# Moving three weight loads and the exponentials within the opening convolution of a residual-block kernel

## The chip, the cores and the metric

The kernel runs on one core of a Trainium2 chip. The metric is the device time of one execution in microseconds (us). The figure for a version is the median of its runs.

## What is computed

The input x has 32 batches of 64 rows of 1024 float32 values. Four layers are added to it, one after the other. `id0` to `id3` are integers, one per batch.

```python
# 0: a long convolution along the 1024 values, one filter K[h] per row h, cut at a length per batch
P = dtA[:, :, None] * arange(1024)               # 64 rows x 64 complex states x 1024 positions
K = 2 * einsum('hn,hnl->hl', Ct, exp(P)).real    # the 64 filters
x = x + mask(id0) * (causal_conv(x, K) + x * D[:, None])
# 1 and 2: a 1024x1024 matrix per batch, chosen among 16
x = x + einsum('bsi,boi->bso', x, w1[id1])
x = x + einsum('bij,bkj->bik', x, w2[id2])
# 3: a gated feed-forward layer (1024 -> 2752 -> 1024) with low-rank additions chosen per batch
x = x + down(silu(gate(x)) * up(x))
```

## The kernel before

**Stages.** The rows of x are cut into 4 chunks of 8 batches (512 tokens). The kernel first does the whole of layer 0 for all batches (`convolution`, L1128 to L1445); the part of it that belongs to the first chunk is added to x in SBUF, the rest is written to DRAM (`cd`). Then layers 1 and 2 follow for the first chunk (`adapter`, L297): each of its 16 pairs of layer and batch needs 8 weight tiles of 128x1024 float32 (0.52 MB each), 128 in all. Then come the feed-forward layer of chunk 0, and the other chunks.

**The filters.** They are made on the chip in nine groups of 4, 4, 8, 8, ... rows (`GROUPS`). Position is split as 32 a + b, and a filter is a small matmul of one factor for `a` with another for `b`. For a group g, `kernels(g)` (L1311) does this:

- GpSimd multiplies out the exponents (`rho`) and the angles (`r`) (`powers`, L1224).
- ScalarE (ACT) takes the exponential of rho (`sizes`, L1241).
- VectorE (DVE) brings the angles into the sine's range (`reduced`, L1172).
- ACT takes the cosine as an Abs and a Sin (`cosine`, L1181), and two more sines (L1324, L1326). Exponential and sine need different function tables, and a table load stands between them.
- DVE multiplies sizes, sines and factors together: `et` and `gt`; the last product is L1336.
- TensorE (PE) makes the filters from them (`pk`, L1341 and L1350), ACT copies these out (`ks`, L1359), and ACT's DMA queue stores them to DRAM (`kp`, L1361).

Two groups are made ahead. The third is started in the middle of the first four rows, and so on: while `convolve` works on a group, the second group after it is made (`more`, L1437). The tile scheduler lays the instructions of all engines out from its own estimate of times, and a `tc.issue_after(i)` puts what stands within it behind instruction i. `behind(done, g)` (L1237) does so for the g-th instruction of a list, or does nothing where g is out of range. In the version before, the exponentials of groups 2 and 3 stand behind the store of group 1 (L1244); those of later groups have no such rule.

**The convolution.** `convolve` (L1367) takes four rows at a time, "a four" (16 fours; the four at row 44 is `ha = 44`). The queue of SyncE (SP) issues its DMAs in order:

- `uf`: the inputs of the four (0.52 MB, two buffers), L1371.
- `hk`: the filters of the first two rows as Toeplitz tiles, read from `kp` with overlapping rows (1.05 MB, three buffers), L1380.
- then weights of the adapter stage by `fetch`, L1389.
- `hk` of the other two rows (the second half-four), and again weights.

PE multiplies each half-four in 16 matmuls of two passes (`pc`, L1396, 32 records in the profile); in the middle of some fours the small `pk` matmuls of a later group come between (`between()`, L1392). DVE masks the result into `tmp` (L1403), GpSimd adds the first chunk's part to x (L1411) and writes the rest to `cd` (L1414, L1415).

**Weights ahead.** `first_weights` (L178) lists 36 of the adapter stage's 128 weight tiles that have a buffer before that stage begins: 9 of the rotating pool, 20 in their own places, 7 in places that become free when the last filters are made. Each `next` on it issues one. Eight go out with the first four (`FIRST_LOADS`, L1373), one with every later four, and a second one with each of the last five (`MORE_LOADS = 5`). The remaining 8 follow behind the last four.

Of the kernel before, what the change touches and what calls it, by code (L numbers as in the profile page):

```python
# [11 lines left out]
AF = mybir.ActivationFunctionType  # L12
# [8 lines left out]
B, H, L = 32, 64, 1024  # L21
# [14 lines left out]
LEFT_AT = 11  # L36
LATE = 7
FIRST_LOADS = 8
MORE_LOADS = 5
ROTATING = 9  # L40
HA = 4
SEG = 2
# [1085 lines left out]
def convolution(tc, cst, consts, xt, xf, ssm, lens, x0, cd, ps_tile, fetch, places):  # L1128
# [10 lines left out]
    nc = tc.nc  # L1139
    with ExitStack() as ctx:  # L1140
# [27 lines left out]
        def tt(o, a, b, op):  # L1168
            nc.vector.tensor_tensor(o, a, b, op)
            return o  # L1170

        def reduced(theta, k):  # L1172

            nc.vector.tensor_scalar(k, theta, 1.0 / TWO_PI, MAGIC, ALU.mult, ALU.add)
            nc.vector.tensor_scalar(k, k, MAGIC, None, ALU.subtract)
            for part in (C1, C2, C3):
                nc.vector.scalar_tensor_tensor(theta, k, -part, theta, ALU.mult, ALU.add)  # L1177
            nc.vector.tensor_scalar(theta, theta, PI_IN, -PI_IN, ALU.min, ALU.max)
            return theta

        def cosine(o, r, k):  # L1181

            nc.scalar.activation(k, r, AF.Abs)
            nc.scalar.activation(o, k, AF.Sin, scale=-1.0, bias=col(CO_HALF))
# [27 lines left out]
        def big(g, tag, pool, pairs):  # L1212

            n = GROUPS[g]
            t = pool.tile([P, (1 + pairs) * HG * LQ], F32, tag=f"b{tag}", name=f"b{tag}{g}")
            if pairs:
                return t[:, : 2 * n * LQ].rearrange("p (i h l) -> p i h l", i=2, h=n)
            return t[:, : n * LQ].rearrange("p (h l) -> p h l", h=n)

        def over_l(g, ap):  # L1220
            h0, n = sum(GROUPS[:g]), GROUPS[g]
            return ap[:, h0 : h0 + n].unsqueeze(2).to_broadcast([P, n, LQ])

        def powers(g, v, pool, tag):  # L1224

            o = big(g, tag, pool, True)
            for i in range(2):
                at_ = cst[:, CO_LVAL + i * LQ : CO_LVAL + (i + 1) * LQ]
                at_ = at_.unsqueeze(1).to_broadcast([P, GROUPS[g], LQ])
                with behind(raised, len(raised) - 1 if g > 1 else -1):  # L1230
                    last = nc.gpsimd.tensor_tensor(o[:, i], over_l(g, v), at_, ALU.mult)
            raised.append(last.ins)
            return o

        sized, made, raised, stored = [], [], [], []

        def behind(done, g):  # L1237

            return tc.issue_after(done[g]) if 0 <= g < len(done) else ExitStack()

        def sizes(g):  # L1241
            rho = powers(g, x, s2, "rho")

            with behind(stored, 1 if g in (2, 3) else -1):  # L1244
                done = nc.scalar.activation(rho, rho, AF.Exp)
            sized.append(done.ins)
            return rho
# [5 lines left out]
        nc.vector.scalar_tensor_tensor(x, ea, -1.0, dt, ALU.mult, ALU.mult)  # L1253
        tt(y, aim, dt, ALU.mult)
        rhos = {g: sizes(g) for g in range(2)}

        t, em, ep = small(), small(), small()
# [29 lines left out]
        re, im = slice(0, NS), slice(NS, P)  # L1287
# [23 lines left out]
        def kernels(g):  # L1311

            h0, n = sum(GROUPS[:g]), GROUPS[g]
            rho = rhos.pop(g) if g in rhos else sizes(g)
            r = powers(g, y, s2, "r")
            k, co = big(g, "k", s1, True), big(g, "co", s1, True)

            with tc.issue_after(made[0]) if g == 1 else ExitStack():
                reduced(r, k)
            si = big(g, "si", s1, False)  # L1320

            with behind(stored, g - 1 if g < 3 else -1):
                cosine(co, r, k)
                nc.scalar.activation(si, r[:, 0], AF.Sin)  # L1324

                nc.scalar.activation(co[im, 1], r[im, 1], AF.Sin)  # L1326
            gt, et = big(g, "gt", s2, False), big(g, "et", s2, False)
            if g == 1:
                done = nc.gpsimd.tensor_tensor(et, co[:, 1], rho[:, 1], ALU.mult)
                raised.append(done.ins)  # L1330
            else:
                tt(et, co[:, 1], rho[:, 1], ALU.mult)
            tt(co[:, 0], co[:, 0], over_l(g, fc), ALU.mult)
            tt(si, si, over_l(g, fs), ALU.mult)
            tt(si, si, co[:, 0], ALU.add)
            done = nc.vector.tensor_tensor(gt, si, rho[:, 0], ALU.mult)  # L1336
            made.append(done.ins)

            ps = ps_tile(f"pk{g}")[:LQ, : n * LQ].rearrange("a (h b) -> a h b", b=LQ)
            for i in range(n):  # L1340
                nc.tensor.matmul(  # L1341
                    ps[:, i],
                    gt[:, i, :],
                    et[:, i, :],
                    start=(i == 0),
                    stop=False,
                    skip_group_check=True,
                )

            nc.tensor.matmul(  # L1350
                ps[:, :, 0],
                cst[:, CO_SEL : CO_SEL + LQ],
                dskip[:, h0 : h0 + n],
                start=False,
                stop=True,
                skip_group_check=True,
            )
            ks = s2.tile([LQ, HG, LQ], F32, tag="ks", name=f"ks{g}")
            nc.scalar.copy(ks[:, :n], ps)  # L1359
            kp = kps[h0 : h0 + n]  # L1360
            done = nc.scalar.dma_start(  # L1361
                kp[:, P:].rearrange("h (a b) -> a h b", b=LQ), ks[:, :n]
            )
            stored.append(done.ins)
            return kp

        def convolve(kp, row, ha, between):  # L1367


            uf = s3.tile([P, HA, KT, B], F32, tag="uf", name=f"uf{ha}", bufs=2)  # L1370
            nc.sync.dma_start(uf, xf[:, ha : ha + HA])  # L1371
            if ha == 0:
                fetch(FIRST_LOADS)  # L1373
            tmp = g0_2.tile([P, HA, KT * B], F32, tag="tmp", name=f"tmp{ha}")
            for i in range(0, HA, 2):
                hk = s3.tile([P, 2, L], F32, tag="hk", name=f"hk{ha + i}")

                for j in range(0, 2, 1 if ha == 0 else 2):
                    n = 1 if ha == 0 else 2
                    nc.sync.dma_start(  # L1380
                        hk[:, j : j + n],
                        bass.AP(
                            tensor=kps.tensor,
                            offset=kp[row + i + j : row + i + j + 1, 1:2].offset,
                            ap=[[1, P], [KROW, n], [1, L]],
                        ),
                    )

                if ha and (i == 0 or ha >= H - HA * MORE_LOADS):  # L1389
                    fetch(1)  # L1390
                if i:
                    between()  # L1392
                ps = ps_tile(f"pc{ha + i}").rearrange("p (i t) -> p i t", i=2)
                for j in range(2):
                    for d in range(KT):
                        nc.tensor.matmul(  # L1396
                            ps[:, j, d * B :],
                            hk[:, j, d * P : (d + 1) * P],
                            uf[:, i + j, : KT - d, :].rearrange("p k b -> p (k b)"),
                            start=(d == 0),  # L1400
                            stop=(d == KT - 1),
                        )
                tt(  # L1403
                    tmp[:, i : i + 2, :],
                    ps,
                    maskf.unsqueeze(1).to_broadcast([P, 2, KT * B]),
                    ALU.mult,
                )
            xv = x0.rearrange("p k (b h) -> p k b h", h=H)[:, :, :, ha : ha + HA]
            tv = tmp.rearrange("p i (k b) -> p k b i", b=B)[:, :, :BC, :]  # L1410
            nc.gpsimd.tensor_tensor(xv, xv, tv, ALU.add)  # L1411
            co = g0.tile([P, NCK - 1, HA * KT, BC], F32, tag="co", name=f"co{ha}")
            tv = tmp.rearrange("p i (k c b) -> p c (i k) b", k=KT, b=BC)[:, 1:]
            nc.gpsimd.tensor_copy(co, tv)  # L1414
            nc.gpsimd.dma_start(  # L1415
                cd.rearrange("c p g e -> p c g e")[:, :, ha // HA],
                co.rearrange("p c i b -> p c (i b)"),
            )


        ready = [kernels(0), kernels(1)]

        lnf = g0.tile([P, B], F32, tag="lnf", name="lnf")
# [187 lines left out]
```

## Time and profile before

| | |
|---|---|
| median of 3 runs | 2308.88 us (2307.97 to 2309.78) |
| profiled execution, and its span | 2305.76 us, 2304.1 us |
| PE busy | 2244.8 us, 97% of the span |
| DVE, ACT, POOL (GpSimd) busy | 1322.2, 379.5, 272.3 us |
| moved by DMA | 684.96 MB, mean 297 GB/s |
| first and last matmul of the convolution (L1396) | 29.2 and 189.2 us |
| PE in L1396 | 151.2 us, 1024 records, mean 309 ns of one |
| landing of an hk (34 DMAs) | 5.5 / 8.8 / 10.4 us, min / median / max |
| chain that ended last | PE 80%, DMA 11%, DVE 4%, issue 3% |

The page cuts the span into 40 equal slices of 57.6 us; a digit is the busy share of an engine in tenths, and the line of GB/s is what DMA moved. A timeline has one instruction or a run of like ones to a line: its start, its time, the engine, the line of the code, what it writes from what, how many; in brackets is how long the engine stood idle before it, and what ended that. A table of stretches has, for each stretch, its length, then the busy us and number of instructions of PE, PEld (weight loads of PE), DVE, ACT and POOL, and then the granted clock of PE, the share of DMA and its GB/s. `SPq` and `ACTq` are the DMA queues of SP and ACT.

### The profile page before, as it was taken

Reading aid. Unit: us, or ns where it says so; the run is one execution under the profiler, and the core shown is the slowest. Engines: PE = TensorE matmul, PEld = TensorE weight load, DVE = VectorE, ACT = ScalarE, POOL = GpSimd, SP = SyncE. Lnnn points to the kernel's source line nnn. Section 1 sums busy time; section 2 is a strip of 40 time slices with the busy share of each in tenths; the row PEclk is TensorE's granted clock in tenths of the full one; section 3 lists DMA queues with packets and bytes.
Section 4 is the critical chain, followed back from the end, with each engine's and each line's share of the span. In section 5 each row is a group of like instructions: output and inputs, shape, how many; then the busy total and the mean of one; then the engine's idle time right before and its main releaser. Section 6 shows DMA issues by size and latency. Waiting matters only on the chain.

```text
span 2304.1 us, 53703 instructions
## 1 busy us (share of the span) xinstructions
PE 2244.8 (97%) x21690; PEld 1863.6 (81%) x21690; DVE 1322.2 (57%) x2791; ACT 379.5 (16%) x822; POOL 272.3 (12%) x388
## 2 busy tenths in 40 slices
PE   4999989999999999999999999999999999999999
PEld 4996557787677789688779889688779889799998
DVE  7511138577447776546535676546535676477585
ACT  4300001011001112122102212122002212121220
POOL 4423004112001221000000011000000011100000
PEclk9999999999999999999999999999999999999999
DMA  8999998889988947889998957889998947285582
GB/s 295 373 389 397 407 387 291 315 303 359 362 322 310 350 161 272 298 290 362 359 348 292 361 154 282 297 298 357 359 330 300 361 148 278 90 292 203 195 278 68
DMA packets 201802, 684.96 MB, mean 297 GB/s; under 512 B 26178, under 2 KB 28482, under 8 KB 201042
## 3 DMA queue, kind: packets, MB, share of 16 engines
q1 hardware_dynamic: 169714, 590.77, 69.9%
q0 software_dynamic: 25184, 82.37, 9.6%
q10 hardware_dynamic: 6656, 8.39, 1.0%
q8 instruction: 171, 2.80, 0.5%
q14 instruction: 77, 0.63, 0.1%
HBM read 614.02 MB, written 67.40 MB: 296 GB/s over the span
## 4 chain that ended last, share of the span: by engine, by line
PE 80%; DMA 11%; DVE 4%; issue 3%; POOL 1%; ACT 0%; SPq 0%; POOLq 0%; ACTq 0%; DVEq 0%
PE pq L662 29%; PE po L1061 23%; PE pa L304 12%; DMA wa<-in_w 7%; PE pf L571 6%; PE pc L1396 5%; PE pr L795 3%; PE pe L454 2%; DMA sums<-kept 1%; DMA wa<-sums 1%; DMA hk<-kp 1%; PE pl_d L425 1%; DVE br L1177 0%; DMA wr<-in_wr 0%; DMA wf<-in_wg 0%
## 5 line engine op out<-in xcount | busy, mean ns | idle before, releaser
L304 PE MATMUL pa<-wa,x 128*32 128x256 f32 x7760 | 447.8, 380 | 18.2 <-DMA wa<-in_w 16.0
L662 PE MATMUL pq<-xd,wa 128*128 128x128 f32 x3360 | 415.6, 275 | 0.4
L304 PEld LDWEIGHTS pa<-wa,x 128*32 128x32 f32 x7760 | 241.6, 110 | 208.1 <-DMA wa<-in_w 48.2
L662 PEld LDWEIGHTS pq<-xd,wa 128*128 128x128 f32 x3360 | 394.9, 192 | 1.1 <-DMA wa<-sums 1.1
L662 PE MATMUL pq<-xd,wb 128*128 128x128 f32 x2520 | 324.1, 276 | 0.1
L662 PEld LDWEIGHTS pq<-xd,wb 128*128 128x128 f32 x2520 | 300.7, 192 | 4.0 <-DMA wb<-parts 0.3
L314 DVE STREAM_TRANSPOSE y<-pa 128x512 f32<-128x512 f32 x64 | 45.9, 716 | 284.0 <-PE pa L304 275.2
L1061 PE MATMUL po<-act,wd 128*128 128x256 f32 x640 | 168.6, 386 | 0.0
L1061 PE MATMUL po<-actd,s 128*128 128x256 f32 x640 | 164.4, 379 | 0.0
L1061 PE MATMUL po<-actd,wd 128*128 128x256 f32 x640 | 164.3, 379 | 0.0
L353 POOL DMA_INDIRECT bgu<-in_bgu,rows x44 | 52.5, 1193 | 915.1 <-PE pe L454 823.6
L1396 PE MATMUL pc<-uf,hk 128*128 128x256 f32 (+7 forms) x1024 | 151.2, 309 | 8.2 <-DMA hk<-kp 7.0
L1396 PEld LDWEIGHTS pc<-uf,hk 128*128 128x128 f32 x1024 | 146.4, 192 | 12.5 <-DMA hk<-kp 5.0
L571 PE MATMUL pf<-xd,wf 128*128 128x256 f32 x640 | 150.6, 381 | 0.0
L1061 PEld LDWEIGHTS po<-act,wd 128*128 128x128 f32 x640 | 117.8, 190 | 29.9 <-issue 14.6
L480 DVE TENSOR_TENSOR s<-wd 128x256 f32<-128x256 f32 x80 | 33.8, 423 | 182.8 <-PE po L1061 182.6
L1061 PEld LDWEIGHTS po<-actd,s 128*128 128x128 f32 x640 | 121.5, 190 | 16.7 <-DVE s L481 0.3
L1061 PEld LDWEIGHTS po<-actd,wd 128*128 128x128 f32 x640 | 121.6, 190 | 16.5
L571 PEld LDWEIGHTS pf<-xd,wf 128*128 128x128 f32 x640 | 120.8, 190 | 17.2
L1093 ACT COPY uo<-po 128x256 f32<-128x256 f32 x48 | 17.9, 372 | 623.7 <-PE po L1061 621.6
L571 PE MATMUL pf<-xd,s 128*128 128x256 f32 x480 | 114.4, 381 | 2.9 <-DVE act L605 1.6
L571 PEld LDWEIGHTS pf<-xd,s 128*128 128x128 f32 x480 | 90.3, 190 | 18.4 <-DVE act L605 3.6
(235 smaller groups left out, 2567.4 us busy)
## 6 DMA issues: line engine op xcount, KB each, us to landing
wa<-in_w SPq DMA_DIRECT2D x485, 512.0 KB, 7.2
wa<-sums SPq DMA_DIRECT2D x210, 512.0 KB, 5.8
wb<-parts SPq DMA_DIRECT2D x120, 384.0 KB, 5.4
wd<-in_wd SPq DMA_DIRECT2D x80, 512.0 KB, 7.0
wb<-in_wq SPq DMA_DIRECT2D x90, 384.0 KB, 6.2
hk<-kp SPq DMA_DIRECT2D x30, 1024.0 KB, 8.9
sums<-kept POOLq DMA_DIRECT2D x30, 1024.0 KB, 7.3
wf<-in_wg SPq DMA_DIRECT2D x20, 512.0 KB, 6.6
```

The source lines that it names most:

```text
L304: nc.tensor.matmul(acc[i * S : (i + 1) * S, s * 256 : (s + 1) * 256], xs[c][:, kt, lo + s * S : lo + (s + 1) * S], wt[:, i * 256 : (i + 1) ...
L314: nc.vector.transpose(y, acc)
L353: nc.gpsimd.indirect_dma_start(out=t, out_offset=None, in_=table, in_offset=bass.IndirectOffsetOnAxis(ap=at_, axis=0),)
L425: nc.tensor.matmul(ps[pair(j)], at[:, i, pair(j)], x_i[:, 2 * H * j : 2 * H * (j + 1)], start=(i == 0), stop=(i == n - 1),)
L454: nc.tensor.matmul(ps[:, at_ * 2 * H : (at_ + 1) * 2 * H], bt[pair(j), g], tms[table][pair(j)], start=(g == 0), stop=True, skip_group_chec ...
L480: nc.vector.tensor_add(s1, a21, a22)
L571: nc.tensor.matmul(ps, ws[j][:, kt, :], xb[j][:, kt, :], start=start and kt == 0, stop=kt == KH - 1, skip_group_check=True,)
L662: nc.tensor.matmul(ps[:, to * TQ : (to + 1) * TQ], w[i][:, k, :], xb[:, j, SLOT[i], k, :], start=start and k == 0 and to == 0, stop=k == K ...
L795: nc.tensor.matmul(ps, wts[i][:, kt, :], xs[c][:, kt, :], start=(kt == 0), stop=(kt == KT - 1),)
L1061: nc.tensor.matmul(pss[j], *term, start=(s0 == m0 and i == 0 and home[j] % 2 == 0), stop=(end and i == len(terms) - 1 and not late), skip_ ...
L1093: nc.scalar.copy(u1, p1)
L1396: nc.tensor.matmul(ps[:, j, d * B :], hk[:, j, d * P : (d + 1) * P], uf[:, i + j, : KT - d, :].rearrange("p k b -> p (k b)"), start=(d == ...
```

## The change

Two things are moved; no operation is added or taken away.

- Weight loads: the fours at rows 4, 8 and 12 issue two, one right behind the other, both between the two hk loads. A second one at the end is left only in the fours at rows 56 and 60.
- Exponentials: those of groups 4 to 8 now stand behind the last sine of the preceding group (`turned`). Those of groups 2 and 3 stay where they were.

```diff
-MORE_LOADS = 5
+MORE_LOADS = 3
...
-        sized, made, raised, stored = [], [], [], []
+        sized, made, raised, stored, turned = [], [], [], [], []
...
         def sizes(g):
             rho = powers(g, x, s2, "rho")
-            with behind(stored, 1 if g in (2, 3) else -1):
+            with behind(*((stored, 1 if g > 1 else -1) if g < 4 else (turned, g - 1))):
                 done = nc.scalar.activation(rho, rho, AF.Exp)
             sized.append(done.ins)
             return rho
...
-                nc.scalar.activation(co[im, 1], r[im, 1], AF.Sin)
+                done = nc.scalar.activation(co[im, 1], r[im, 1], AF.Sin)
+            turned.append(done.ins)
...
-                if ha and (i == 0 or ha >= H - HA * MORE_LOADS):
+                first, last = ha <= HA * MORE_LOADS, ha > H - HA * MORE_LOADS
+                if ha and i == 0:
+                    fetch(1 + first)
+                elif ha and last:
                     fetch(1)
```

## Prediction

> **What bounds the kernel now.** I read the 40 slices of the page first, then the stretches of the opening, then TensorE's (PE's) and the DMA queue's (SPq's) instructions in order of time. In the page, DMA is nearly full only in the first six slices (57.6 us each, so up to 346 us).
>
> ```profile
> PE   4999989999999999999999999999999999999999
> DMA  8999998889988947889998957889998947285582
> GB/s 295 373 389 397 407 387 291 315 303 359 362 322 310 350 161 272 298 290 362 359 348 292 361 154 282 297 298 357 359 330 300 361 148 278 90 292 203 195 278 68
> ```
>
> The change touches only the convolution, which ends at 189.2 us. Its stretches, with DMA share and GB/s in the last columns:
>
> ```profile
> 20.00:60.00 40.00, 30.49 (x242) 29.27 (x243) 30.06 (x53) 20.75 (x33) 21.87 (x27) 1.00 0.81 292
> 60.00:100.00 40.00, 40.00 (x305) 39.03 (x303) 28.01 (x47) 16.46 (x25) 18.02 (x21) 1.00 0.99 370
> 100.00:140.00 40.00, 39.23 (x299) 38.13 (x298) 5.53 (x8) 0.72 (x2) 9.68 (x12) 1.00 0.99 366
> 140.00:190.00 50.00, 47.17 (x328) 45.28 (x327) 7.61 (x11) 0.00 (x0) 11.87 (x16) 1.00 1.03 410
> 265.00:325.00 60.00, 50.50 (x744) 22.67 (x739) 7.04 (x10) 1.32 (x2) 0.00 (x0) 1.00 1.02 406
> ```
>
> Three regimes: until 60 us DMA has room (292 GB/s of some 410); from 60 to 140 PE sets the pace (39.2 to 40.0 of 40 us busy); from 140 to 190 DMA is at its ceiling and PE loses 2.83 us. After that the first adapter stage waits for weights (265 to 325 us: PE 50.5 of 60, DMA 406 GB/s). The granted clock is 1.00 in all of them.
>
> PE's waits inside the convolution stand in brackets:
>
> ```profile
> 46.30 0.69 PE L1341 MATMUL pk<-bet,bgt 128*32 128x32 f32 x16 [0.36 <-DVE bgt L1336]
> 56.67 0.66 PE L1341 MATMUL pk<-bet,bgt 128*32 128x32 f32 x16 [0.33 <-DVE bgt L1336]
> ...
> 115.88 18.72 PE L1396 MATMUL pc<-uf,hk 128*128 128x256 f32 x128 [0.77 <-DMA hk<-kp]
> ...
> 149.94 9.36 PE L1396 MATMUL pc<-uf,hk 128*128 128x256 f32 x64 [0.77 <-DVE tmp L1169]
> 159.76 9.36 PE L1396 MATMUL pc<-uf,hk 128*128 128x256 f32 x64 [0.47 <-DMA hk<-kp]
> 170.02 9.36 PE L1396 MATMUL pc<-uf,hk 128*128 128x256 f32 x64 [0.90 <-DMA hk<-kp]
> 179.81 9.36 PE L1396 MATMUL pc<-uf,hk 128*128 128x256 f32 x64 [0.43 <-issue]
> ```
>
> They sum to 4.03 us. The one at 149.94 is a late hk too, whatever name stands there: that hk was issued at 140.43 and took 9.4 us. An hk is issued when PE frees its buffer, two half-fours (9.36 us) before its use; the median landing is 8.8 us. So hk is on time by half a microsecond, and a weight queued ahead of it (0.52 MB, 1.28 us at 410 GB/s) makes it late.
>
> **Part one: three weight loads move.** Nothing is added or removed: 28 loads go out between the convolution's steps in both versions. The second loads of the fours at channels 44, 48 and 52 (issued at 135.78, 145.18, 155.30) go to those at 4, 8 and 12, right behind the first loads there (29.07, 45.43, 52.80).
>
> What the late end gains: fours 44 to 52 then ask for 3.5 MB each (uf 0.52, hk 2.10, weight 0.52, cd 0.39) in 9.33 us, or 378 GB/s, as the fours from 60 to 140 do, where PE waited for hk once. Doubled fours remain at 56 and 60, asking 4.05 MB, or 434 GB/s. The first doubled four (44) delayed hk of 48, so 56 should delay 60: of 0.77 + 0.47 + 0.90 + 0.43 = 2.57 us I keep the last wait, taken as 0.5. Gain 2.1 us (bounds 0.7 to 2.6). The wait at 115.88 arose among single loads and stays.
>
> What the early end costs:
> - Four 4: the second load (about 29.6) stands ahead of the hk issued at 35.64, which is used at 46.96, 11.3 us later. Even its 8.8 us plus 1.28 fits: nothing.
> - Four 8: its two loads go out right behind the hk at 44.86 and fill a hole (205 GB/s from 40 to 45, 165 from 45 to 50). The next hk (45.97) took 10.4 us and is used at 57.31; 11.3 us are there: nothing.
> - Four 12: here cover is thin. The next hk (56.38, 9.6 us) lands at 66.0 and is used at 66.6. In the built order of the changed program the second load waits for the completion semaphore that the store of group 3's kernels used, so SP stops there until that store has landed, with the hk behind it. I put that store at 50.5 (below); such stores took 5.9 to 9.0 us, so SP is free between 56.4 and 59.5, against PE freeing the hk's buffer at 56.0. At best DMA has emptied meanwhile and nothing is late; at worst hk is 3 us late and PE waits 2.5. I take 0.4, near the good end: SP stood only at its head, and DMA went on with the 2.1 MB issued before.
>
> **Part two: exponentials wait for sines.** ScalarE (ACT) now, group 3 of the kernels:
>
> ```profile
> 35.91 1.28 ACT L1245 ACT_TABLE_LOAD   x1 [1.77 <-DVE bgt L1336]
> 37.97 0.63 ACT L1245 ACTIVATE brho<-brho 128x512 f32<-128x512 f32 x1 [0.77 <-POOL brho L1231]
> 38.50 0.35 ACT L1359 COPY ks<-pk 32x256 f32<-32x256 f32 x1
> 38.88 0.31 ACTq L1361 DMA_DIRECT2D kp<-ks  x1
> 39.84 0.63 ACT L1183 ACTIVATE bk<-br 128x512 f32<-128x512 f32 x1 [1.00 <-DVE br L1178]
> 40.49 1.28 ACT L1324 ACT_TABLE_LOAD   x1
> 41.78 0.42 ACT L1324 ACTIVATE bsi<-br 128x256 f32<-128x256 f32 x1
> ```
>
> Group 4's exponentials (35.91 to 38.60) lie ahead of group 2's store and cost group 3's sines a table load. With them behind the sines, group 2's store goes at about 37.1 instead of 38.88, so its hk (44.86) leaves up to 1.8 us sooner, unneeded by PE before 51.6. Group 3's sine runs at 40.49, 1.29 us sooner; its last DVE product moves from 45.83 to about 43.9, as the order also puts it ahead of GpSimd's add, next to which such products took 1.0 instead of 0.42 us. PE wanted it at 45.93: the 0.36 at 46.30 goes. Likewise group 4's product leads by some 3 us and the 0.33 at 56.67 goes. Gain 0.69 (bounds 0 and 0.69). What is late next is PE itself.
>
> The price: group 3's copy now stands behind group 4's first sine. That sine waits for DVE's reduction, done near 47.5, then 0.63, 1.28 and 0.42 us: the store goes at about 50.5 instead of 49.10. Its hk is wanted at 62.56: cover 12 us less a landing under 9. Group 4's store falls behind group 6's exponentials, to about 62 instead of 59.57; its hk goes out at 81.74. Both are hidden, save through the semaphores. The number of table loads stays 12: the last two groups shared one, now the second and third do.
>
> The row says 1.28 us for a load, and the sine starts 0.01 us after it. The Trainium skill ("ScalarE: Activation LUTs", section "What ACT_TABLE_LOAD costs") adds a drain of 1.38 us, 2.66 us a switch. By it group 3's sine would gain 2.66 us, and PE still only its 0.36; the sum is unchanged.
>
> **Sum.** 2.1 + 0.69 - 0.4 = 2.4 us off the convolution. It carries on: the adapter stage behind it is short of DMA, every byte before it is the same, and at 175 us DMA is backlogged in both versions; from 325 us on PE's chain leads and nothing there moves (the order of instructions is the same on all engines). The profiled execution took 2305.76 us around a span of 2304.1; it becomes 2303.4. The median of the runs shown, 2308.88, lies 3.12 us higher: 2306.5 us.
>
> **Rivals.**
> - Only bytes shift, 15%: the early room is used, but the late fours fall to PE's pace with other hk late, and what was won at 140 to 190 goes in new waits near 60 and 115. The 0.69 remains: 2308.2. For it: single loads waited at 115.88 too.
> - All waits go, 20%: the 4.03 us and a queue shorter at 175 by up to 0.9 us (hk landings of 9.1 to 10 us there against 8.6 in the single fours): 2304.0. For it: the hole at 40 to 50 held room for more than three loads.
> - Slower, 10%: SP's stops at the kernels' stores. Beside group 3's, the program has a uf load of four 20 waiting for group 4's store and one of four 28 for group 5's. If stores land 9 us or more after issue, SP stands 2 to 3 us each time and hk, with half a microsecond to spare, is late each time: 3 x 2.3 = 6.9 us of new waits, 2306.5 + 6.9 = 2313.4. It decides once a store is still out over 1 us after PE has freed the buffer. Against it: 5.9 and 8.2 us landings.
> - The forecast holds 55%.
>
> **Numbers.** Predicted 2306.5. The best bounds give 2.6 + 0.69 + 0.9 more from the queue and 0.77: 2303.9; the worst 0.7 + 0 - 2.5: 2310.7. The runs spread 0.9 us either way, so the range is 2303.0 to 2310.8. 0.2% is 4.6 us, about what a measurement can tell from no change. Faster by more needs all waits gone and a little luck: 0.26. Within: 0.62. Slower by more, the third rival and some unseen stall: 0.12.
>
> **What would show it.** Right: no wait of L1341 at 46 and 56; PE's waits for hk after 140 us falling from 2.57 to below 1; DMA at 40 to 50 us far above 185 GB/s and at 140 to 160 below 410; the convolution's last matmul near 186.8 instead of 189.2. Wrong: waits for hk at 60 to 100 us, or SP idle before the second load of four 12 beyond 59 us; or an opening that is shorter and a later stage that gives it back.

## The result, and the profile after

The changed kernel takes 2314.26 us (median of 22 runs, 2309.44 to 2323.44), the kernel before 2309.9 us in the 22 runs beside them: a ratio of 1.0021, 95% interval 1.0012 to 1.0029 (2.8 to 6.7 us). It is slower by some 4.4 us, outside the range of the prediction.

The profiled execution of the changed kernel has a span of 2314.0 us, 9.9 us over the one of before. In the code its lines stand a little lower: pc L1401, hk L1382, uf L1373, pk L1343, weights L170 as before.

The slices of the page, as for before:

```profile
PE   5999989999999999999999999999999999999999
DMA  8999998879998947879997957789997957285572
GB/s 309 347 380 394 408 399 288 316 288 361 362 332 303 350 165 268 302 286 360 352 353 289 350 160 271 303 293 356 349 348 291 355 153 276 88 297 204 193 277 69
```

DMA moves more in the first slice (309 for 295 GB/s) and less in the second (347 for 373): the early hole was filled, and then something kept DMA from its work. The stretches of the opening say where (same columns as in the prediction):

```profile
20.00:60.00 40.00, 31.37 (x243) 30.28 (x244) 29.98 (x51) 17.91 (x30) 20.07 (x26) 1.00 0.86 312
60.00:100.00 40.00, 36.91 (x282) 35.96 (x281) 25.68 (x47) 19.46 (x28) 17.70 (x20) 1.00 0.90 333
80.00:100.00 20.00, 20.00 (x152) 19.53 (x151) 11.94 (x22) 7.08 (x12) 6.55 (x7) 1.00 0.86 303
100.00:140.00 40.00, 37.61 (x288) 36.52 (x287) 5.53 (x8) 0.50 (x2) 11.27 (x14) 1.00 0.99 381
140.00:190.00 50.00, 49.00 (x338) 47.69 (x338) 6.92 (x10) 0.22 (x1) 11.97 (x15) 1.00 1.00 383
```

From 140 to 190 us PE is now busy for 49.00 us instead of 47.17, as was hoped. But from 60 to 100 it lost 3.09 us where it had lost none, and from 80 to 100 DMA ran at 303 GB/s, where it had run at 365. PE's timeline names the instructions (in brackets the idle time ahead of each and what ended it):

```profile
46.30 9.44 PE L1401 MATMUL pc<-uf,hk 128*128 128x256 f32 x64
55.67 0.69 PE L1343 MATMUL pk<-bet,bgt 128*32 128x32 f32 x16
57.07 9.36 PE L1401 MATMUL pc<-uf,hk 128*128 128x256 f32 x64 [0.67 <-DMA hk<-kp]
69.52 9.36 PE L1401 MATMUL pc<-uf,hk 128*128 128x256 f32 x64 [3.09 <-DMA hk<-kp]
105.56 14.17 PE L1401 MATMUL pc<-uf,hk 128*128 128x256 f32 x96 [2.12 <-DMA hk<-kp]
...
168.28 14.09 PE L1401 MATMUL pc<-uf,hk 128*128 128x256 f32 x96 [0.74 <-DMA hk<-kp]
182.62 7.63 PE L1401 MATMUL pc<-uf,hk 128*128 128x256 f32 x50 [0.26 <-issue]
```

Every gain of the forecast is there: no wait ahead of pk, none at 116 us, and the waits after 140 us fell from 2.57 to 1.00. Against them stand three new waits, at the second halves of the fours at rows 8 and 12 and the first half of the four at row 28: 0.67, 3.09 and 2.12 us. All waits of the convolution come to 7.09 us instead of 4.31 (the 4.03 of the prediction and 0.28 at 35.89, ahead of a pk, which is gone too), so 2.78 more. The convolution takes 163.41 us instead of 159.96; nearly all the rest of this 3.45 is its first half-four, 7.10 us instead of 6.40. At 326 us, where the adapter stage's PE chain ends, the changed kernel is 3.1 us behind. The other 6.8 us of the two spans come later, up to 1821 us, as single late weights that fall anywhere; below, a second profile of the kernel before shows the same.

The two big waits have one origin, seen in SP's DMA queue (start, time, line, what is issued):

```profile
52.14 0.34 SPq L170 DMA_DIRECT2D wa<-in_w  x1
60.78 0.34 SPq L170 DMA_DIRECT2D early<-in_w  x1
61.23 0.55 SPq L1382 DMA_DIRECT2D hk<-kp  x1
...
88.89 0.38 SPq L1382 DMA_DIRECT2D hk<-kp  x1
97.44 0.33 SPq L1373 DMA_DIRECT2D uf<-in_xf  x1
97.83 0.45 SPq L1382 DMA_DIRECT2D hk<-kp  x1
```

And before:

```profile
52.80 0.34 SPq L170 DMA_DIRECT2D wa<-in_w  x1
56.38 0.37 SPq L1380 DMA_DIRECT2D hk<-kp  x1
...
90.51 0.34 SPq L1371 DMA_DIRECT2D uf<-in_xf  x1
90.94 0.42 SPq L1380 DMA_DIRECT2D hk<-kp  x1
```

In the changed kernel, from 52.5 to 60.8 and from 89.3 to 97.4, SP issues nothing. In the first hole the second load of four 12 waits, and behind it the hk that PE wants at 66.4; in the second, uf of four 28 and the hk behind it. The waits of SP for stores of kernels from 40 to 110 us, first after and then before (what waits, for what, us in total, times, longest):

```profile
SPq L1373 <- DMA kp<-ks: 12.3, 2, 8.1
SPq L170 <- DMA kp<-ks: 8.1, 1, 8.1
SPq L1382 <- DMA kp<-ks: 2.6, 1, 2.6
```

```profile
SPq L1380 <- DMA kp<-ks: 3.1, 1, 3.1
```

An hk reads kp, the stored kernels; a load of weights and a load of uf have nothing to do with it. They wait for those stores because of the built program: the DMAs of SP and ACT signal on eight completion counters in turn, and a DMA is held until the one eight places before it has landed. The changed program has a store of kernels eight places ahead of each of these. The records of the trace bear this out: the DMAs of SP and ACT carry eight semaphore numbers in all, group 3's store and the held load of four 12 both carry 112, group 5's store and the uf of four 28 both 111. And the stores are late, which ACT's timeline shows:

```profile
36.82 0.31 ACTq L1363 DMA_DIRECT2D kp<-ks  x1
40.18 0.40 ACT L1325 ACTIVATE bsi<-br 128x256 f32<-128x256 f32 x1
41.65 1.28 ACT L1246 ACT_TABLE_LOAD   x1
49.88 0.63 ACT L1183 ACTIVATE bk<-br 128x512 f32<-128x512 f32 x1 [6.30 <-DVE br L1178]
52.52 0.31 ACTq L1363 DMA_DIRECT2D kp<-ks  x1
```

```profile
86.80 0.63 ACT L1183 ACTIVATE bk<-br 128x512 f32<-128x512 f32 x1 [3.62 <-DVE br L1178]
87.34 0.34 ACT L1361 COPY ks<-pk 32x256 f32<-32x256 f32 x1
87.71 0.31 ACTq L1363 DMA_DIRECT2D kp<-ks  x1
```

The same two stores before:

```profile
49.10 0.31 ACTq L1361 DMA_DIRECT2D kp<-ks  x1
...
81.84 0.32 ACTq L1361 DMA_DIRECT2D kp<-ks  x1
```

Group 2's store goes 2.06 us sooner than before (36.82 for 38.88). Group 3's stands behind group 4's absolute value and first sine, which wait for DVE until 49.88: it goes at 52.52 instead of 49.10 and takes 8.2 us to land. Group 5's stands behind group 8's exponentials and absolute value: 87.71 instead of 81.84, landing in 9.7 us.

### The profile page after: what moved, and what is told of

Read it like the earlier page. It is cut to its first block, busy times and chain, and to the rows that moved or that the text cites. A ratio compares the mean times of both kernels' runs of the same rounds, so it can differ in the third digit from the quotient of the medians.

```text
span 2314.0 us, 53708 instructions
## 1 busy us (share of the span) xinstructions
PE 2247.7 (97%) x21690; PEld 1866.5 (81%) x21690; DVE 1319.8 (57%) x2791; ACT 379.8 (16%) x822; POOL 265.2 (11%) x388
## 4 chain that ended last, share of the span: by engine, by line
PE 76%; DMA 12%; DVE 5%; issue 4%; POOL 1%; ACT 1%; SPq 0%; POOLq 0%; ACTq 0%; DVEq 0%
PE pq L662 28%; PE po L1061 23%; PE pa L304 12%; DMA wa<-in_w 6%; PE pf L571 5%; PE pc L1401 3%; PE pr L795 3%; DMA wa<-sums 2%; DMA sums<-kept 2%; PE pe L454 1%; DVE br L1177 1%; PE pl_d L425 1%; DMA hk<-kp 1%; DMA wf<-in_wg 1%; DMA wr<-in_wr 0%
## 5 line engine op out<-in xcount | busy, mean ns | idle before, releaser
L1401 PE MATMUL pc<-uf,hk 128*128 128x256 f32 (+7 forms) x1024 | 152.0, 311 | 11.7 <-DMA hk<-kp 11.2
L1401 PEld LDWEIGHTS pc<-uf,hk 128*128 128x128 f32 x1024 | 147.2, 194 | 16.0 <-issue 7.3
L353 POOL DMA_INDIRECT bgu<-in_bgu,rows x44 | 45.7, 1039 | 919.1 <-PE pe L454 827.2
```

Of the source, the lines that this page charges most:

```text
L353: nc.gpsimd.indirect_dma_start(out=t, out_offset=None, in_=table, in_offset=bass.IndirectOffsetOnAxis(ap=at_, axis=0),)
L1401: nc.tensor.matmul(ps[:, j, d * B :], hk[:, j, d * P : (d + 1) * P], uf[:, i + j, : KT - d, :].rearrange("p k b -> p (k b)"), start=(d == ...
```

## The experiments

Two theories. **Stop:** the loss is SP's standing behind the late stores of groups 3 and 5. **Bytes:** 0.52 MB more at each of three early fours makes an hk late wherever it falls, whatever the stores do. One table first; each kernel's edit and expectation follow. "Waits" are PE's waits from 50 to 110 us in its one profile, "convolution" the time from its first to its last matmul there (160.0 before and 163.4 changed, in the first profiles), "stores" the issue of group 3's and group 5's. The ratio is to the runs of before beside it.

| kernel | median us (runs) | ratio, 95% interval | waits us | convolution us | stores at us |
|---|---|---|---|---|---|
| before, again (c_before) | 2311.15 (12) | 1.0009 [0.9999, 1.0019] | 0.82 | 161.7 | 49.2, 81.9 |
| changed, again (c_after) | 2314.29 (11) | 1.0027 [1.0016, 1.0038] | 5.24 | 162.7 | 52.9, 88.1 |
| loads alone (e_weights) | 2313.99 (12) | 1.0018 [1.0008, 1.0028] | 3.27 | 161.4 | 49.3, 85.4 |
| exponentials alone (e_exps) | 2312.47 (11) | 1.0013 [1.0001, 1.0024] | 1.66 | 161.6 | 52.7, 86.3 |
| changed, early stores (e_stores) | 2309.57 (11) | 1.0002 [0.9989, 1.0015] | 2.91 | 167.3 | 47.1, 81.2 |
| changed, stores by GpSimd (e_pool) | 2316.63 (10) | 1.0039 [1.0026, 1.0051] | 2.53 | 166.7 | 53.2, 89.2 |
| before, early stores (e_before_stores) | 2310.17 (12) | 0.9996 [0.9986, 1.0005] | 0.90 | 160.4 | 49.1, 77.2 |
| three loads later, none early (e_none) | 2312.07 (11) | 1.0014 [1.0005, 1.0022] | 0.33 | 163.6 | 49.1, 81.8 |
| only group 5's store early (e_store5) | 2314.34 (12) | 1.0021 [1.0009, 1.0034] | 3.74 | 164.9 | 52.9, 82.3 |
| only group 3's store early (e_store3) | 2314.29 (11) | 1.0019 [1.0006, 1.0031] | 4.38 | 162.7 | 47.1, 88.6 |
| doubled fours 4, 8, 16 (e_sixteen) | 2320.40 (6) | 1.0049 [1.0029, 1.0068] | 6.52 | 164.9 | 53.0, 87.9 |
| doubled fours 4, 8 (e_two) | 2313.58 (12) | 1.0007 [0.9995, 1.0019] | 2.26 | 162.1 | 52.8, 87.8 |
| the same, early stores (e_two_stores) | 2308.86 (12) | 0.9998 [0.9987, 1.001] | 0.92 | 161.2 | 47.7, 78.0 |
| loads alone, early stores (e_weights_stores) | 2309.59 (12) | 0.9994 [0.9981, 1.0007] | 1.74 | 162.0 | 49.1, 79.1 |

**How far one profile can be trusted.** Both kernels unchanged, once more.

> The kernel before once more, unchanged, to learn how much of a single profile is the kernel and how much the execution. If a profile stands for its kernel, the convolution (first to last matmul of the convolved channels) is 160 us again within 1, the four late waits for hk after 140 us come to 2 to 3 us, and no wait over 0.5 us stands between 57 and 110 us. If the transfers differ from one execution to the next, the convolution is longer by as much as the execution is longer than 2305.76, and single waits move: then only medians of many runs, and waits that come back at the same instruction, may be read.

> The changed kernel once more, unchanged. Stop theory (SyncE's queue stands until the stores of the kernels of groups 3 and 5 have landed): waits over 1.5 us come back at the second half of four 12 (about 69 us) and of four 28 (about 105 us), with SyncE's queue named for kp<-ks at the second load of four 12 and at uf of four 28, both again 5 to 8 us; time 2313 to 2315. Bytes theory (three more weights in the early stretch make hk late wherever it happens to fall): the sum of the waits from 50 to 110 us is again 5 to 6 us, but at other instructions, and SyncE's stops have moved or shrunk.

The same code as before gave a ratio of 1.0009, so a tenth of a per cent can't be told from nothing, and its second profile has a span of 2314.2 us against 2304.1. Of these 10.1 us only 1.6 and 1.7 are there at 361 and 490 us; most of the rest has come by 1304 us, from scattered late weights. The span of one profile says little, then. The waits inside the convolution come back better: late ones 2.80 us after 2.57, and nothing over 0.5 us from 57 to 110 us. But its convolution took 161.65 us, more than the 1 us from 160 that was expected; the changed kernel's second took 162.73. So the first profiles lie 3.45 us apart here and the second ones 1.08. The changed kernel's second profile:

```profile
68.94 9.36 PE L1401 MATMUL pc<-uf,hk 128*128 128x256 f32 x64 [1.37 <-DMA hk<-kp]
105.63 1.65 PE L1401 MATMUL pc<-uf,hk 128*128 128x256 f32 x8 [2.29 <-DMA hk<-kp]
```

The wait of four 28 (ahead of its first half) is there again within 0.2 us (2.12, 2.29), that of four 12 at the same instruction with less than half the size (3.09, 1.37). The late waits are 1.22 us.

**Each half of the change alone.** e_weights keeps the exponentials of before, e_exps the loads of before.

> Only the weight loads move; exponentials as before. Stop theory (SP's queue stands at a DMA whose completion semaphore was last taken by a store of kernels): group 3's store goes at about 49 us instead of 52.5 and lands near 57, so SP is held at the second load of four 12 only about 1 us past the point at which PE frees the hk buffer; PE waits 0.5 to 1.5 us for the second hk of four 12 instead of 3.09, and up to 1 us at four 28 instead of 2.12. Convolution, first to last matmul: 159 to 161 us (before 160.0, after 163.4). Bytes theory (the weights themselves hold up the hk behind them): the wait at four 12 stays at 2.5 to 3.5 us, convolution 161 us or more.

> Only the exponentials move; weights as before. Stop theory: group 3's store is not in the way of four 12 here (the uf of four 16 shares its semaphore, issued at 62 us), so no wait at four 12; group 5's store goes at about 87 instead of 81.8 us, and the first hk of four 28, which must wait for its semaphore, leaves near 97 instead of 91: PE waits about 2 us at four 28. The waits of 0.36 and 0.33 at the small matmuls go, the waits beyond 140 us stay (2.57). Convolution 160 to 162 us, time 0 to 3 us above before. Bytes theory: no wait at four 28, convolution 159.3, time 0.7 us below before.

Each half alone is slower than before, by 0.18% and 0.13% (4.2 and 3.0 us). Together they cost 0.21% and 0.27% in the two measurements of the changed kernel; with intervals of a tenth of a per cent either way, these runs can't tell whether the halves share a loss or add up. The loads alone have a stop of 6.8 us at uf of four 28, since group 5's store went at 85.43 there, and one of 2.9 us at four 12. But their profile speaks against the stop at four 28: after it PE waited for nothing, its hk (95.75) was in time, and the 1.37 us at 94.10 (where the profile names DVE) stand at a half-four whose hk was issued at 83.99, ahead of the stop; 0.94 at 68.79 stands at four 12. The exponentials alone have no wait at four 12, but 0.87 us at 92 and, behind a stop of 3.3 us at the hk of four 28, 0.79 at 103, where about 2 were expected; their late waits stay at 2.69 us, since the late fours are as before.

**The stops taken away.** e_stores puts the sines of every group behind the store of the group before; e_pool sends the stores over GpSimd's queue, which has other counters.

```diff
-            with behind(stored, g - 1 if g < 3 else -1):
+            with behind(stored, g - 1):
```

```diff
-            done = nc.scalar.dma_start(
+            done = nc.gpsimd.dma_start(
```

> The changed kernel, but from group 3 on the sines of a group stand behind the store of the group before, so that this store is issued as soon as its kernels are made: group 3's at about 47 us instead of 52.5, group 5's at about 79 instead of 87.7. The queue and the semaphores stay. Stop theory: stores land before SP reaches what shares their semaphores; waits at four 12 and four 28 fall below 1 us each, convolution 157.5 to 159.5 us, time 4 us below the changed kernel and 1 to 3 below the one before. Bytes theory: the wait at four 12 stays near 3 us, convolution 161 or more.

> The changed kernel, but the stores of the kernels go through GpSimd's DMA queue, which has semaphores of its own; the hk loads still wait for the stores that they read. Stop theory: SP is held at no weight or uf load by a store any more; the waits of 3.09 at four 12 and 2.12 at four 28 fall below 1 each, convolution 157.5 to 159.5 us (after 163.4), time 4 us below the changed kernel, unless GpSimd, which now stands at each store, delays something else. Bytes theory: the 3.09 stays, convolution 162 or more.

With early stores the median is that of before, 4.7 us under the changed kernel. In its profile uf of four 28 goes out at 94.69 without a stop and nothing waits near 105 us; at four 12 the stop shrinks to 3.8 us and 1.85 us of waiting remain. That profile does not show the gain, though: its convolution took 167.3 us, the longest of all, where 157.5 to 159.5 were expected, as 4.65 us of waits stand after 140 us (2.72 of them at 188), and it reaches the end of the adapter stage (326 us before the change) 5.1 us later than the changed kernel's first profile. The execution that was profiled took 2313.32 us, 3.75 over the median. The gain rests on the medians alone. e_pool also lost both stops (0.89 us at four 12, none at four 28), and was yet the slower kernel: its profile waits 1.18 us at 114, 1.00 at 134 and 2.68 at 185 us, and GpSimd is busy 276.2 us instead of 265.2. Its stores are as late as in the changed kernel. Why the hk are late there is not settled: with both stops gone the stop theory expected 4 us less, unless GpSimd held something else up, and the time rose. Which of the two it is no run tells; as a proof of the stops it fails.

**Early stores without the change, and the loads moved the other way.** e_before_stores is before with the diff of e_stores. e_none is before with the loads of fours 44, 48 and 52 put behind those of the last four (`ha >= H - HA * 2`, no doubled fours early).

> The kernel before, with the sines of every group of kernels put behind the store of the group before it (as the first groups have it already), so that the stores of groups 3 to 5 go earlier and not behind a later group's table work; weights as before. Nothing is left out. Stop theory: before already has three stops at hk for kp<-ks of 13.4 us together, which cost nothing visible, so this gains at most 1 us: 2308 to 2311. If instead the earlier stores were worth the 4.7 us that they gave the changed kernel, whatever the weights: 2304 to 2306. Bytes theory: no change beyond the noise, as the bytes are the same.

> The kernel before, with the three weight loads of the fours 44, 48 and 52 put behind the convolution's last loads and none of them early; exponentials as before. Nothing is left out. Stop theory: SyncE's stops are those of before, so the early waits are too; the late waits fall from 2.6 us to about 1, and the time is 2307 to 2310, unless the adapter stage wants the three weights sooner than they come, which would show as waits for them at 200 to 330 us. Bytes theory: the same bytes are due before the adapter stage ends, so what the convolution wins is given back there: 2308.5 to 2311, the same as before.

Before has nothing to gain from early stores (0.9996; 1 us under its own repeat), so what they gave the changed kernel is not a gain that every kernel would have; it repairs something that the change brought in. e_none fits neither theory: its late waits fell only to 2.25 us, one hk at 112 us was 2.14 us late, and by 326 us it is 7.3 us behind. PE's waits for weights between 190 and 330 us grew from 10.1 to 12.0 us: a load that goes late is not free.

**One store at a time, and the weight at another four.** e_store5 has `g - 1 if g < 3 or g > 5`, e_store3 `g - 1 if g < 5` in the line of e_stores. e_sixteen has `first = ha in (HA, 2 * HA, 4 * HA)`.

> The changed kernel, with the sines of groups 6 to 8 alone put behind the store of the group before, so that group 5's store no longer stands behind the table work of group 8; group 3's store stays at 52.5 us. Nothing is left out. Stop theory: the wait at four 28 (2.1 and 2.3 us at about 105 us in two profiles of the changed kernel) goes, as uf of four 28 is issued when its buffer is free (about 91 us) and not at 97.4, and the DMA share from 80 to 100 us is back above 0.95 (0.86 and 0.85); the wait at four 12 stays at 1.4 to 3.1; time 2 us below the changed kernel, 2311 to 2313. Bytes theory: the wait at 105 us stays above 1 us or comes back within the next two fours in the same size, and the time is 2313 to 2315.

> The changed kernel, with the sines of groups 3 and 4 put behind the store of the group before, so that group 3's store goes at about 47 us instead of 52.5; group 5's stays late. Nothing is left out. Stop theory: SyncE's stop ahead of the second load of four 12 shrinks from 6.6 to 8.1 us to at most 4, and the wait at about 69 us falls below 1.4 us, while the wait at 105 us stays at 2.1 to 2.3; time 1 to 2 us below the changed kernel, 2312 to 2314. Bytes theory: the stop shrinks but the wait at 69 us stays at 1.4 us or more, since the weight itself (0.52 MB) stands ahead of the hk; time 2313.5 to 2315.

> The changed kernel with the third of the doubled weights at four 16 instead of 12 (fours 4, 8, 16). Nothing is left out. The hk of four 12's second half now itself takes the place in SyncE's queue that waits for group 3's store, so the stop stays (until about 60.5 us) but the 0.5 MB of the weight behind it are gone. Stop theory: the wait at about 69 us is as in the changed kernel, 1.2 to 3 us. Bytes theory: it falls below 1 us, and a wait of about 1 us comes at four 16 or 20 (75 to 95 us). In both the wait at four 28 depends on which store its uf meets. Time 2312 to 2315.

Each repair leaves the other wait, and only group 5's takes its own away. With group 5's store early, uf of four 28 goes at 95.78, no wait stands near 105 us, DMA from 80 to 100 us is at 357 GB/s, and four 12 still waits 3.11 us. With group 3's early, the stop at four 12 shrinks to 4.0 us, but 1.49 us of waiting remain, no less than in the changed kernel's second profile (1.37), and four 28 waits 1.83: this came out as the bytes theory had it. The medians did not follow: both stay at 2314.3 us, with intervals of 0.12% either way, 2.8 us. One repair was expected to give 2; whether it gives that or nothing, these runs can't tell.

e_sixteen took no byte less and has the longest single stop, 9.7 us; SP's queue around it (uf is not the first in line here, but the second hk of four 24):

```profile
84.95 0.34 SPq L170 DMA_DIRECT2D early<-in_w  x1
95.06 0.38 SPq L1382 DMA_DIRECT2D hk<-kp  x1
95.52 0.64 SPq L1373 DMA_DIRECT2D uf<-in_xf  x1
```

```profile
102.14 20.06 PE L1401 MATMUL pc<-uf,hk 128*128 128x256 f32 x127 [3.76 <-DMA hk<-kp]
```

An hk that is itself held until 95.06 costs PE 3.76 us. The kernel is the slowest of all, 2320.4 us, where 2312 to 2315 was expected by both theories; but the profiled execution is the fastest of its six, 2312.48 us, so this wait does not explain that median. At four 12 the weight is gone and the stop remains (hk at 60.75): 1.31 us of waiting.

**What is stop and what is bytes.** e_two gives up only the doubled four 12 (`first = ha <= HA * 2`, `last = ha >= H - HA * MORE_LOADS`), e_two_stores adds the early stores; e_weights_stores is the loads alone with them.

> The changed kernel with the doubled four 12 given up (4 and 8 early, 52, 56 and 60 late); the exponentials, and so the late stores of groups 3 and 5, as in the changed kernel. Nothing is left out. It differs from the version with the early stores by the stores alone. Stop theory: the stores are what costs, so with their landing still at about 60.7 us SyncE stands again, at whatever DMA of four 12 or 16 meets it, and again near four 24 or 28: waits over 1 us at 66 to 70 and at 92 to 106 us, time 2312 to 2315. Bytes theory: without the doubled four 12 the waits from 50 to 110 us fall below 2 us together, and the time is 2308 to 2311, as with early stores.

> The changed kernel with two doubled fours early (4 and 8) and three late (52, 56, 60), and the sines of every group behind the store of the group before: the version that the runs so far point to, without the doubled four 12 and with the stores early. Nothing is left out. Stop theory: no stop of SyncE ahead of fours 12 and 28, waits from 50 to 110 us below 1.5 us together, late waits 1.5 to 2 us, and a time of 2306 to 2309. Bytes theory: 0.7 to 0.9 us at 57 to 59 us stays, so do other waits of half a microsecond to a microsecond, and the time is that of the kernel before, 2309 to 2311.

> The three loads moved as in the change, the exponentials as before, and the sines of every group behind the store of the group before. Nothing is left out. It differs from the version with the loads alone (2314.0 us) by the stores alone. Stop theory: SyncE's stop of 6.8 us at uf of four 28 goes and the wait near 94 us (1.4 us) with it; a stop at four 12 remains small; time 2309 to 2311.5. Bytes theory: the waits from 50 to 110 us stay at 3 us together, at these or other places, and the time stays at 2313 to 2315.

With the stop and no weight at four 12 (e_two; hk at 60.12) nothing waits there, though 1.31 us did in e_sixteen; with the weight and hardly a stop (2.6 us in e_weights_stores) 0.97 us; with both 1.37 to 3.11. At four 28 the first hk goes out at 95.1 to 98.0 us where a store holds it or the uf ahead of it, and PE waits 2.12 and 2.29 us in the changed kernel, 1.83 with group 3's store early, 1.60 in e_two, 0.79 in e_exps and nothing in e_weights (hk at 95.75); in the kernels with group 5's store early on ACT's queue there is no wait there. SP's waits in e_weights_stores from 40 to 110 us:

```profile
SPq L1380 <- DMA kp<-ks: 4.8, 2, 2.8
SPq L170 <- DMA kp<-ks: 2.6, 1, 2.6
```

Three pairs differ by the stores alone. Changed: 1.0021 and 1.0027 against 1.0002. Loads alone: 1.0018 against 0.9994. In both, intervals lie apart, if narrowly ([1.0016, 1.0038] and [0.9989, 1.0015]; [1.0008, 1.0028] and [0.9981, 1.0007]); that of the changed kernel's first measurement, from 1.0012, overlaps. Fours 4 and 8: 1.0007 against 0.9998, which overlap. So the medians show that the order with early stores takes back part of the loss, by their middle values nearly all of it. Two things they do not show. One is the way: that the time goes through SP's stops is seen for the waits of the changed kernel, but e_pool lost the stops and stayed slow, and the profile of the loads alone has the stop at four 28 without a wait. The other is that it is the stores: the same rule also moves ACT's sines, and no run moved the stores alone on ACT's queue. The profiles of the pairs agree with the medians twice (with early stores the end of the adapter stage comes 1.1 and 1.6 us sooner) and not in the changed kernel's pair (5.1 later). e_two_stores has 2.77 us of late waits, where 1.5 to 2 were expected.

No version is faster than before: the best of the four with early stores, 0.9994, holds 1 in its interval. All four hold it, with and without the moved loads; of the seven kernels with group 5's store at 85 us or later six are slower with an interval above 1, and e_two's holds 1 too ([0.9995, 1.0019]). Group 5's store is not the whole: e_store5 and e_none, with it at about 82 us, are slower than before as well.

## Why the prediction was wrong, by its own steps

- **Late fours, gain 2.1:** right in kind and nearly in size. 2.57 us of waits became 1.00 and 1.22 in the two profiles; 383 GB/s from 140 to 190 us instead of 410.
- **pk waits, gain 0.69:** right, both are gone in both profiles, and so is one of 0.28 us at 35.89, which the sum of 4.03 had left out. Without its table load group 3's sine starts 0.54 us after the absolute value began (39.64, 40.18) instead of 1.94 (39.84, 41.78): 1.40 us, near the 1.28 of the row and not the 2.66 that the prediction quotes beside it.
- **Fours 4 and 8 at nothing:** four 4 yes, four 8 no. "11.3 us are there", but the hk, issued at 45.74, took 11.2 to land behind one weight more: 0.67 us, and 0.56 to 0.88 at that place in all seven profiles with three doubled fours and the moved exponentials, with late and early stores alike. The text added a weight's 1.28 us for four 4 and not here, where 10.4 + 1.28 is 11.7 already; and with the pk waits gone PE was there at 56.40, 0.9 us sooner. That points to bytes, but e_two, with the same doubled fours 4 and 8, waits for nothing there, so it stays open.
- **Four 12, "I take 0.4, near the good end":** this step failed. The stop was named, its counter and its store too, and bounded by 2.5 us; it took 3.09 and 1.37 us. Two estimates under it were short. The store was put at 50.5 and went at 52.52, since DVE's reduction came at 49.9 instead of 47.5; and 8.2 us of landing made SP free at 60.8, beyond the 59 that the text gave as the sign of being wrong. The reason for the good end, that DMA has enough to do meanwhile, was true of DMA (406 to 420 GB/s from 52 to 60 us) and beside the point: the hk itself stood in the queue, behind a weight.
- **Group 5's store:** not priced in the forecast at all. The text followed group 3's and 4's stores, and called them hidden "save through the semaphores". Group 5's, which fell behind group 8's table work, moved by 5.9 us, and PE waited 2.12 us at four 28, in a place where it had waited for nothing. That is the omitted term: the text names the uf of four 28 in a rival only, and argues there with landings of 5.9 and 8.2 us, though group 5's own store took 9.0 before.
- **The rival "slower"** was given 10% and 2313.4 us, three stops of 2.3 each, against 2314.26 measured. It names the mechanism that the trace shows: four 12 and four 28 paid, four 20 did not (its uf was held for some 4 us and nothing was late). That its number came so near is partly luck: two stops paid, not three, and 0.67 us stands elsewhere. Its condition, a store still out 1 us after PE has freed the buffer, was met by 4.7 us at four 12.
- **Sum:** by the profile, new waits 0.67 + 3.09 + 2.12 + 0.21 less before's 0.28 + 0.36 + 0.33 + 0.77 and the 1.57 late ones is 2.78 us; the last matmul of the convolution came 2.88 us later, and 3.1 us were found at 326 us. The measured 4.4 us is a little more, but its interval begins at 2.8, so nothing need be missing; the next section has what may add to it. The range's upper end was also added up wrongly: 2310.7 and the spread of 0.9 make 2311.6, not 2310.8, which the measured time exceeds as well.
- The median shown of before, of 3 runs, stood at 2308.88; 22 runs gave 2309.9. This 1 us is not the error.

## What the runs showed that was not expected

**A long wait can cost more than its length.** In the 16 profiles' convolutions, none of the 20 waits of 1.0 to 1.6 us ahead of a matmul changed the granted clock. Of 11 waits of 1.83 us and more, 7 were followed by 3.0 to 3.4 us at half clock, which costs another 1.5 to 1.7 us. The first four microseconds after the 3.11 us wait in e_store5 (last columns: clock, DMA share, GB/s), and the two half-fours, the first of which began in them:

```profile
70.00:74.00 4.00, 3.85 (x16) 3.69 (x16) 0.11 (x1) 0.00 (x0) 1.99 (x3) 0.57 1.03 415
```

```profile
70.15 11.02 PE L1401 MATMUL pc<-uf,hk 128*128 128x256 f32 x64 [3.11 <-DMA hk<-kp]
```

11.02 us for 64 records that otherwise take 9.36. In both profiles of the changed kernel the clock happened to hold, after 3.09, 2.12 and 2.29 us. If seven in eleven of its long waits fall into it in other runs, that is some 2 us more on average (2 x 7/11 x 1.65), an estimate that would bring the 3.1 to 5.2, on the other side of the measured 4.4. The mean granted clock of every run bears on this: it is below 1.000 in 28 of the 33 runs of the changed kernel, in 4 of its 11 with early stores, and in 27 of 132 runs of the kernel before. On average the changed kernel loses 0.09% of the clock more, or about 2.1 us (an estimate from clocks of three decimals). So most of its executions have a stretch at half clock that neither of its profiles shows. It is still not the cause by itself: its five runs at 1.000 take 2313.9 us on average, no less than those at 0.999 (2314.1). The Trainium skill ("TensorE: Matmul & The Clock Gate", section "HAM oscillation — how this bites in real kernels") warns of idle gaps over about 3.4 us. Here gaps of 1.83 to 3.11 us were enough in six profiles and one of 3.09 us was not, so as a bound below which the clock holds the figure does not fit this case.

**Small stores land slowly under load.** 32 KB of kernels took 8.2 and 9.7 us to land here, as long as 1 MB of hk beside them (8.6 us median from 40 to 100 us).

## What to carry to other kernels

A DMA moved to an earlier place is also moved nearer to the DMAs whose completion it must share: look in the built order at which DMA it takes its counter from (eight places ahead in this program), and when that one lands, before calling a hole in the traffic free. When two parts of a change are priced, follow every small store that the second part delays to whoever is held by it, not only to whoever reads its data. And a queue in order makes the most urgent load pay for the least urgent one ahead of it: a weight that is wanted 100 us later may cost nothing in bandwidth and still make PE wait.
